# Two attentions of a transformer kernel: value products placed between the two banks of a step's second half of scores

## The chip, the cores and the metric

The kernel runs on one core of a Trainium2 chip. The metric is the device time of one execution in microseconds (us), as the median of several runs. TensorE (PE) multiplies matrices into PSUM, its accumulation memory of eight banks; VectorE (DVE), ScalarE (ACT) and GpSimd (POOL) do the elementwise work and the reductions; SyncE (SP) issues most DMAs. PEld is the loading of TensorE's weights. Each engine runs its own instructions in order and waits for the others at semaphores.

## The reference

The input x has 16 batches of 512 tokens with 128 features. Two layers follow each other, each an attention and a feed-forward part, with a layer norm ahead of each part and the sum with x behind it. Both attentions have 16 heads of 8 features; the first is causal, the second is not.

```python
    x = L0_attn_hidden_states
    x = x + _L0_attn_ref(_layernorm(x, axis=-1), ...)   # 16 heads, causal mask, projection
    x = x + _L0_ffn_ref(_layernorm(x, axis=-1), ...)    # 8 experts, the best 2 of each token
    x = x + _L1_attn_ref(_layernorm(x, axis=-1), ...)   # 16 heads, no mask
    x = x + _L1_ffn_ref(_layernorm(x, axis=-1), ...)    # gated, values rounded to a 4-bit grid

# an attention, q, k, v of shape (batch, head, token, 8):
        w = jnp.einsum('bhnd,bhmd->bhnm', q, k) * jax.lax.rsqrt(float(D))
        mask = jnp.tril(jnp.ones((S, S), dtype=jnp.float32))     # first attention only
        w = jnp.where(mask > 0, w, NEG)
        w = jax.nn.softmax(w, axis=-1)
        attn = jnp.einsum('bhnm,bhmd->bhnd', w, v)
```

## The kernel before, in words

One function, `attention(layer)`, emits both attentions. The 16 heads of a batch are worked off in 4 groups of 4 heads, so that there are 64 groups, and each group in NC = 4 steps, one for each block of 128 keys (`kc`). A count `now` runs over all 256 steps of an attention; a batch has 16 of them.

A step has the following parts. Every matmul of queries and keys uses 64 rows of PE's array: heads lie on two strips of 64 partitions, and the two strips (`j` = 0 and 1) go into two different PSUM banks. In the profile they are "64*128".

- `score(kc, pairs)` multiplies the keys of one block with the queries into two banks (`ps_sc`), one for each strip, and ACT takes the exponentials of each bank into `pt`. In the first attention POOL then clears what lies behind the mask (L981). `parts` cuts the scores of a step: two halves where two heads of a strip don't fit one bank, and a single part otherwise. In the second attention every step has two halves of 512 columns. In the first, step 0 has two halves of 512 columns and step 1 two of 384; steps 2 and 3 have a single part, of 2 x 256 and 2 x 128 columns.
- `row_max` computes the row maxima for the group that is LEAD = 3 groups ahead: PE writes the scores into two banks (`ps_max`), in the first attention adds a mask (a bf16 matmul with `ident_bf` and `mask_bf`, 128*128), and DVE reduces them (L923). A step's maxima come in the same one or two parts; the first of them is issued at the end of the step before, by `first_maxima`, the rest inside the step.
- `attend(kc)` is the value product of the step behind: four matmuls (`ps_av<-pt,va`, 128*32, which the profile counts as eight), one for each head of the group, each on its own 32 columns of PE's array. They accumulate in one bank over the four steps of a group. Behind the last of them `leave` lets ACT copy the bank to `av_sb`.
- `divide` turns the products of a finished group back (`ps_d`) at step 2 of the next group; DVE takes reciprocals and multiplies.
- Work for other batches is hung onto steps by number, in three tables: `soon` (ahead of the first maxima of a step), `later` (behind the first scores) and `last_of` (behind the last scores). It brings further PE operations: `ps_t`, `ps_qk`, `ps_v`, `ps_mx`, in the first attention also `ps_o` and `ps_n`.

The tiles `ps_sc`, `ps_av`, `ps_mx`, and in part `ps_t`, `ps_qk` and `ps_v`, take turns in a ring of 4 banks (`for_act`), one of which the value product of the group holds nearly all the time. `ps_max`, `ps_d` and the rest take turns in 2 buffers of two banks (`for_dve`).

The order on PE is that of the program: every matmul goes through `mm`, and `in_order` ties it to the one before. In the attentions the lanes of DVE, ACT and POOL are tied in the same way. The order within a step is written out in the loop at the end of `attention`: first scores, the divide (in the second attention it goes into `last_of`), `later`, the rest of the maxima, the second half of the scores, `last_of`, the first maxima of the next step, and the value products of the step behind. Where the second attention has something in `last_of` (`turned`), the products come ahead of the first maxima.

Of the kernel before, what the change touches and what calls it, by code (L numbers as in the profile page):

```python
# [36 lines left out]
def transformer_kernel(  # L37
# [25 lines left out]
    NC = S // P  # L63
# [79 lines left out]
    first = cp.tile([P, NE], F32, name="first")  # L143
# [8 lines left out]
    def in_order(ins, queue="pe", passing=False):  # L152


        if queue in last:
            tc.add_manual_dep(
                ins.ins, last[queue].name,
                mybir.DependencyInfo(
                    mybir.DependencyClass.NoSync, mybir.DependencyReason.DATA
                ),  # L160
                reason="in_order",
            )
        if not passing:
            last[queue] = ins.ins
        return ins
# [129 lines left out]
    def mm(out, lhsT, rhs, start=True, stop=True):  # L295
        return in_order(nc.tensor.matmul(out, lhsT, rhs, start=start, stop=stop))  # L296
# [320 lines left out]
    def attention(layer):  # L617
        causal = layer == 0
# [32 lines left out]
        def for_act(name):  # L651
            return ring["act"](name)
# [246 lines left out]
        def strip(j):  # L899
            return slice(64 * j, 64 * (j + 1))  # L900
# [52 lines left out]
        def main_parts(b, g):  # L953


            hv = halves[b, g // 2]
            va = state[b]["va"]
            pts = {}
            acc = {}

            def score(kc, pairs):
                q0 = kc * P if causal else 0
                n = S - q0
                m = len(pairs)
                tiles = [for_act("ps_sc") for j in range(2)]
                for u, i in enumerate(pairs):
                    p = 2 * (g % 2) + i
                    for j, ps in enumerate(tiles):
                        r = strip(j)
                        mm(  # L970
                            ps[:, u * n : (u + 1) * n],
                            hv["k"][r, p, kc * P : (kc + 1) * P], hv["q"][r, p, q0:S],
                        )
                for j, ps in enumerate(tiles):
                    pt = pool.tile([P, S], F32, tag="pt", name="pt", bufs=12 if causal else 8)
                    act.activation(pt[:, 0 : m * n], ps[:, 0 : m * n], AF.Exp, scale=SCALE)
                    if causal:

                        head = pt[:, 0 : m * n].rearrange("p (u n) -> p u n", u=m)[:, :, 0:P]
                        in_order(  # L980
                            nc.gpsimd.affine_select(  # L981
                                head, head, pattern=[[0, m], [1, P]], base=0,
                                channel_multiplier=-1, compare_op=ALU.is_ge, fill=0.0,
                            ),
                            queue="pool",
                        )
                    for u, i in enumerate(pairs):
                        pts[kc, i, j] = pt[:, u * n : (u + 1) * n]

            def attend(kc):  # L990
                if kc == 0:
                    acc[0] = for_act("ps_av")
                av = acc[0]
                q0 = kc * P if causal else 0
                for i in range(2):
                    for j in range(2):
                        s = 2 * j + i
                        mm(
                            av[32 * s : 32 * (s + 1), q0:S],
                            va[:, kc, NP * j + 2 * g + i, :],  # L1000
                            pts.pop((kc, i, j)),
                            start=kc == 0, stop=kc == NC - 1,
                        )

            def leave():
                t = pool.tile([P, S], F32, tag="av_sb", name="av_sb")
                act.copy(t, acc.pop(0))
                return t

            return score, attend, leave  # L1010

        def divide(b, g, t):

            st = state[b]
            if g == 0:
                st["at"] = pool.tile([P, NC, E], F32, tag="at", name="at")
            ps = for_dve("ps_d")[:, 0, :]
            for c in range(NC):
                cols = slice(c * P, (c + 1) * P)
                turn_to(ps[:, cols], t[:, cols])  # L1020
            p3 = ps.rearrange("p (n k) -> p n k", k=32)
            rec = pool.tile([P, NC * 4, 1], F32, tag="rec", name="rec")
            vec.reciprocal(rec, p3[:, :, D : D + 1])
            at = st["at"].rearrange("p c (j n d) -> p (c j) (n d)", j=2, d=D)
            vec.tensor_tensor(
                at[:, :, 2 * D * g : 2 * D * (g + 1)].rearrange("p m (i d) -> p m i d", d=D),
                p3[:, :, 0:D].rearrange("p (m i) d -> p m i d", i=2),
                rec.rearrange("p (m i) o -> p m i o", i=2).to_broadcast([P, NC * 2, 2, D]),
                ALU.mult,
            )  # L1030
# [32 lines left out]
        def parts(blocks):  # L1063

            return [(0, 1)] if causal and 2 * blocks * P <= S else [(0,), (1,)]

        def max_steps(n):
            if n >= len(groups):
                return []
            b, g = groups[n]  # L1070
            return [
                [(lambda c=c, u=u: row_max(b, g, c, u)) for u in parts(c + 1)]
                for c in reversed(range(NC))
            ]

        def max_done(n, step=None):
            if n < len(groups) and n % 2 == 1:
                at = groups[n][0], (n % G) // 2
                if step is None:
                    part_max(*at)  # L1080
                    put_max(*at)
                else:
                    soon.setdefault(step, []).append(lambda: part_max(*at))
                    later.setdefault(step + (not causal), []).append(lambda: put_max(*at))


        soon, later, last_of = {}, {}, {}
# [125 lines left out]
        behind, left = [], []  # L1213
# [77 lines left out]
        maxima = []  # L1291

        def first_maxima(now):

            for f in soon.pop(now, []):
                f()
            n, kc = divmod(now, NC)
            if kc == 0:
                rows[:] = max_steps(n + LEAD)
            if rows:  # L1300
                maxima[:] = rows.pop(0)
                maxima.pop(0)()
# [3 lines left out]
        for n, (b, g) in enumerate(groups):  # L1306
            nxt = n + LEAD
            score, attend, leave = main_parts(b, g)
            max_done(nxt, NC * (n + 1))
            for kc in range(NC):  # L1310
                now = NC * n + kc
                scores = [lambda u=u: score(kc, u) for u in parts(NC - kc)]
                scores.pop(0)()
                if kc == 2 and left:
                    bb, gg, t = left.pop(0)
                    if not causal:
                        last_of.setdefault(now, []).append(lambda a=(bb, gg, t): divide(*a))
                    else:
                        divide(bb, gg, t)
                    if gg == G - 1 and causal:  # L1320
                        later.setdefault(now + 1, []).append(lambda bb=bb: turn_back(bb))
                        at = now + 3
                        later.setdefault(at, []).append(lambda bb=bb: finish(bb))
                        gate_after(bb, at)
                    elif gg == G - 1:
                        later.setdefault(now + 1, []).insert(0, lambda bb=bb: finish(bb))
                        quantize_after(bb, now + 1)
                for f in later.pop(now, []):
                    f()
                for f in maxima + scores:  # L1330
                    f()
                maxima.clear()
                turned = now in last_of and not causal
                for f in last_of.pop(now, []):
                    f()
                if not turned:

                    first_maxima(now + 1)

                while behind:  # L1340
                    behind.pop(0)()
                if turned:
                    first_maxima(now + 1)
                behind.append(lambda kc=kc, f=attend: f(kc))
            behind.append(lambda b=b, g=g, f=leave: left.append((b, g, f())))
        while behind:
# [499 lines left out]
```

## Time and profile before

| What | Value |
|---|---|
| Median of 3 runs | 2224.25 us (2222.96 to 2224.55) |
| Profiled execution, device time | 2213.31 us |
| Its span, first to last instruction | 2211.6 us |
| Mean granted clock of PE | 0.958 |
| Busy share of the span: PE, PEld, DVE, ACT, POOL | 91%, 46%, 74%, 58%, 44% |
| Step scores in the first attention | 62.3 us to about 760 us |
| Step scores in the second attention | about 1180 us to 1970.7 us |

The two attentions take about two thirds of the span; experts stand between them, and the gated feed-forward part behind them. In the timeline a row is a start, a duration, an engine and an operation with the number of instructions merged into it. Durations of matmuls overlap with what follows, since their ends are modelled: from start to start is the safer reading. Nearly all work of the attentions goes through two helper lines (L296 for PE, L177 for the lanes of the other engines), so that groups have to be told apart by their tiles.

### The profile page before, as it was taken

What the parts mean: (1) busy time and instruction counts of PE and PEld (TensorE: products, weight loads), DVE (VectorE), ACT (ScalarE), POOL (GpSimd) and SP (SyncE); (2) the same over time, 40 slices, a digit from 0 to 9 for tenths busy, and PEclk for the clock granted to TensorE, in tenths of its full rate; (3) what the DMA queues carried; (4) which work ended last, traced back from release to release, by engine and by line L of the source; (5) the groups of instructions that cost most, each with busy time, mean ns of one, the idle gap of its engine ahead of it and who ended that gap; (6) DMA issues with size and microseconds to landing.
All of it is one profiled execution on the core that took longest, in us unless ns stands there. A gap on an engine that the chain in (4) does not pass through costs nothing.

```text
span 2211.6 us, 38195 instructions
## 1 busy us (share of the span) xinstructions
PE 2021.9 (91%) x13141; PEld 1026.8 (46%) x13141; DVE 1633.6 (74%) x3002; ACT 1288.7 (58%) x2549; POOL 979.4 (44%) x1593
## 2 busy tenths in 40 slices
PE   6999999999999939899998999999999999987887
PEld 3454444444444416565763333333333333335565
DVE  5777677777777666468637888888888888828776
ACT  1566666656666623323336777777777777763433
POOL 3454756657465750321204454554545552222331
PEclk6899999999999969999999999999999999998888
DMA  6521223222232024564542222222222222000000
GB/s 178 126 67 62 82 93 105 74 68 79 86 111 75 30 74 121 144 179 124 165 119 89 79 85 75 70 74 72 70 71 86 85 72 70 22 1 10 20 24 24
DMA packets 148735, 180.14 MB, mean 81 GB/s; under 512 B 25647, under 2 KB 112784, under 8 KB 140352
## 3 DMA queue, kind: packets, MB, share of 16 engines
q1 hardware_dynamic: 139614, 160.26, 24.1%
q0 software_dynamic: 8352, 17.20, 2.6%
q8 instruction: 105, 1.72, 0.3%
q14 instruction: 86, 0.70, 0.1%
q10 hardware_dynamic: 578, 0.26, 0.1%
HBM read 116.55 MB, written 58.99 MB: 79 GB/s over the span
## 4 chain that ended last, share of the span: by engine, by line
PE 43%; DVE 9%; ACT 4%; issue 1%; POOL 0%; DMA 0%; ACTq 0%; DVEq 0%; POOLq 0%
PE ps_av L296 11%; PE ps_sc L296 8%; PE ps_max L296 6%; PE ps_h L296 5%; PE ps_y L296 5%; DVE hid L177 4%; ACT pt L177 3%; PE ps_gu L296 3%; DVE mx L923 2%; PE ps_d L299 2%; PE ps_qk L296 2%; PE ps_t L299 1%; PE ps_mx L299 1%; PE ps_v L296 1%; DVE f_rc L177 1%
## 5 line engine op out<-in xcount | busy, mean ns | idle before, releaser
L177 ACT ACTIVATE pt<-ps_sc 128x512 f32<-128x512 f32 (+2 forms) x1792 | 895.4, 572 | 397.1 <-PE ps_sc L296 381.4
L923 DVE TENSOR_REDUCE mx<-ps_max 128x2 f32<-128x1024 f32 (+1 forms) x896 | 993.2, 1143 | 180.2 <-PE ps_max L296 175.6
L296 PE MATMUL ps_sc<-q,k 64*128 64x512 f32 (+3 forms) x2048 | 512.4, 424 | 41.0 <-ACT pt L177 38.7
L296 PE MATMUL ps_av<-pt,va 128*32 128x512 f32 (+3 forms) x4096 | 477.2, 528 | 7.1 <-POOL pt L981 7.0
L296 PE MATMUL ps_max<-k,q 64*128 64x512 f32 (+3 forms) x2048 | 435.2, 412 | 21.6 <-DVE mx L923 12.1
L296 PEld LDWEIGHTS ps_sc<-q,k 64*128 64x128 f32 x2048 | 234.8, 185 | 443.5 <-ACT pt L177 329.9
L981 POOL TENSOR_SCALAR_AFFINE_SELECT pt<-pt 128x128 f32<-128x128 f32 (+1 forms) x768 | 244.9, 331 | 237.6 <-ACT pt L177 221.5
L296 PEld LDWEIGHTS ps_max<-k,q 64*128 64x128 f32 x2048 | 202.1, 189 | 181.3 <-DVE mx L923 54.7
L1538 ACT ACTIVATE h<-ps_h,b1t 128x512 f32<-128x512 f32 x156 | 106.9, 687 | 185.9 <-PE ps_h L296 185.5
L1462 POOL DMA_INDIRECT got<-y_rows,backs x128 | 125.4, 979 | 99.5 <-DMA y_rows<-yt 65.1
L296 PE MATMUL ps_h<-xT,w1t 128*128 128x512 f32 x312 | 153.0, 623 | 13.3 <-ACT h L1538 8.0
L296 PE MATMUL ps_y<-w2t,h 128*128 128x128 f32 x1248 | 146.5, 276 | 0.8 <-DVE yt L1552 0.8
L296 PEld LDWEIGHTS ps_y<-w2t,h 128*128 128x128 f32 x1248 | 142.5, 192 | 3.2 <-issue 2.2
L296 PEld LDWEIGHTS ps_av<-pt,va 128*32 128x32 f32 x4096 | 83.7, 108 | 129.0 <-issue 61.0
L537 POOL DMA_INDIRECT x_rows<-xg,slots x128 | 127.6, 997 | 27.6 <-issue 25.0
L206 POOL TENSOR_TENSOR ln_rstd<-ln_ve,mhalf 128x4 f32<-128x4 f32 x62 | 64.2, 1035 | 157.8 <-DVE ln_nm L177 130.0
L296 PE MATMUL ps_max<-mask_bf,ident_bf 128*128 128x128 bf16 (+1 forms) x768 | 127.2, 249 | 0.0
L177 DVE RECIPROCAL rec<-ps_d 128x16 f32<-128x16 f32 x128 | 32.6, 255 | 108.3 <-PE ps_d L299 108.3
L177 POOL TENSOR_TENSOR hid<-hid,f_sc 128x1408 f32<-128x1408 f32 x16 | 41.4, 2587 | 136.5 <-DVE hid L177 136.5
L177 ACT ACTIVATE hid<-ps_gu 128x352 f32<-128x352 f32 x64 | 29.7, 463 | 123.0 <-PE ps_gu L296 123.0
L296 PE MATMUL ps_gu<-wgT,xqT 128*128 128x352 f32 x128 | 62.8, 579 | 41.1 <-DVE hid L177 41.1
L177 ACT COPY av_sb<-ps_av 128x512 f32<-128x512 f32 x128 | 75.2, 587 | 42.8 <-PE ps_av L296 42.3
(241 smaller groups left out, 2186.8 us busy)
## 6 DMA issues: line engine op xcount, KB each, us to landing
q<-d SPq DMA_DIRECT2D x256, 128.0 KB
k<-d SPq DMA_DIRECT2D x256, 128.0 KB
d<-hi SPq DMA_DIRECT2D x64, 256.0 KB
d<-lo SPq DMA_DIRECT2D x64, 256.0 KB
xt<-x_rows SPq DMA_DIRECT2D x39, 262.0 KB
w1t<-in_w_dram SPq DMA_DIRECT2D x39, 256.0 KB
w2t<-in_w_dram SPq DMA_DIRECT2D x39, 256.0 KB
y_rows<-yt SPq DMA_DIRECT2D x39, 256.0 KB
```

The costliest lines, as they stand in the source:

```text
L177: ins = f(*args, **kw)
L206: in_order(nc.gpsimd.tensor_tensor(rstd, ve, mhalf, ALU.pow), queue="pool")
L296: return in_order(nc.tensor.matmul(out, lhsT, rhs, start=start, stop=stop))
L299: return in_order(nc.tensor.transpose(out, src, ident))
L537: ins = in_order(nc.gpsimd.indirect_dma_start(out=x_rows[:, :], out_offset=bass.IndirectOffsetOnAxis(ap=slots[:, b0 + u, k, c : c + 1], axis=0
L923: nc.vector.tensor_reduce(hv["mx"][:, c, :, p0 : p0 + m], s4, AX.X, ALU.max),
L981: nc.gpsimd.affine_select(head, head, pattern=[[0, m], [1, P]], base=0, channel_multiplier=-1, compare_op=ALU.is_ge, fill=0.0,),
L1462: ins = in_order(nc.gpsimd.indirect_dma_start(out=got[:, c, :], out_offset=None, in_=y_rows[0 : min(NT, NE * (b + 1)) * TS, :], in_offset= ...
L1538: nc.scalar.activation(h[:, f, :], ps, AF.Gelu, bias=t["b1"][:, f : f + 1])
```

## The change

In steps with two halves, the second half of the scores is issued one bank at a time, and the value products of the step behind (`attend`, and `leave` behind the last step of a group) are put between the two banks. Then come `last_of` and the first maxima of the next step. In steps with a single part (steps 2 and 3 of the first attention) the order stays: first maxima, then value products. The special order of `turned` is gone: in the second attention the divide now stands behind the value products, and the first maxima follow it directly. `score` gets an argument for the strips that it computes.

```diff
-            def score(kc, pairs):
+            def score(kc, pairs, strips=(0, 1)):
...
-                tiles = [for_act("ps_sc") for j in range(2)]
+                tiles = [(j, for_act("ps_sc")) for j in strips]
                 for u, i in enumerate(pairs):
                     p = 2 * (g % 2) + i
-                    for j, ps in enumerate(tiles):
+                    for j, ps in tiles:
...
-                for j, ps in enumerate(tiles):
+                for j, ps in tiles:
...
-                scores = [lambda u=u: score(kc, u) for u in parts(NC - kc)]
-                scores.pop(0)()
+                first, *second = parts(NC - kc)
+                score(kc, first)
...
-                for f in maxima + scores:
+                for f in maxima:
                     f()
                 maxima.clear()
-                turned = now in last_of and not causal
+                woven = bool(second)
+                for u in second:
+                    score(kc, u, (0,) if woven else (0, 1))
+                sums, behind[:] = list(behind), []
+                if woven:
+                    for f in sums:
+                        f()
+                    for u in second:
+                        score(kc, u, (1,))
                 for f in last_of.pop(now, []):
                     f()
-                if not turned:
-                    first_maxima(now + 1)
-                while behind:
-                    behind.pop(0)()
-                if turned:
-                    first_maxima(now + 1)
+                first_maxima(now + 1)
+                if not woven:
+                    for f in sums:
+                        f()
```

## The prediction

> **What bounds the kernel now.** I read the page's sections 1 and 4 first, then the table of windows, the waits, and last the timeline of TensorE (PE) inside single steps.
>
> ```profile
> PE 2021.9 (91%) x13141; PEld 1026.8 (46%) x13141; DVE 1633.6 (74%) x3002; ACT 1288.7 (58%) x2549; POOL 979.4 (44%) x1593
> ...
> PE 43%; DVE 9%; ACT 4%; issue 1%; POOL 0%; DMA 0%; ACTq 0%; DVEq 0%; POOLq 0%
> ```
>
> PE is the busiest engine and carries the chain; no DMA stands in it. By stage, from the windows (us; PE, PEld, DVE, ACT, POOL busy):
>
> ```profile
> 400.00:700.00 300.00, 288.99 (x2322) 143.19 (x2320) 223.61 (x503) 188.26 (x416) 184.76 (x429) 0.99 0.26 82
> 1500.00:1750.00 250.00, 239.35 (x1464) 95.65 (x1462) 215.51 (x332) 191.45 (x370) 129.45 (x144) 1.00 0.24 77
> ```
>
> First attention: PE 96%, VectorE (DVE) 75%. Second: PE 96%, but DVE 86%, so little can come off PE there before DVE ends last. Clocks are full. The waits (us, times, longest):
>
> ```profile
> PEld ps_av L296 <- POOL pt L981: 30.8, 89, 2.0
> PE ps_sc L296 <- ACT pt L177: 38.7, 149, 4.5
> PE ps_max L296 <- DVE mx L923: 12.1, 35, 1.1
> ```
>
> The second is the wait the change aims at: the last bank of a step's scores waits for an exponential to free one. An ordinary step of the second attention (start, duration):
>
> ```profile
> 1600.36 1.06 PE L296 MATMUL ps_av<-pt,va 128*32 128x512 f32 x8
> 1601.36 0.50 PE L296 MATMUL ps_sc<-q,k 64*128 64x512 f32 x2
> ...
> 1601.70 0.39 PE L296 MATMUL ps_max<-k,q 64*128 64x512 f32 x2
> ...
> 1601.93 0.39 PE L296 MATMUL ps_sc<-q,k 64*128 64x512 f32 x1
> ...
> 1602.54 0.49 PE L296 MATMUL ps_sc<-q,k 64*128 64x512 f32 x1 [0.21 <-ACT pt L177]
> ...
> 1602.54 0.72 PE L296 MATMUL ps_max<-k,q 64*128 64x512 f32 x2
> ...
> 1603.19 1.07 PE L296 MATMUL ps_av<-pt,va 128*32 128x512 f32 x8
> ```
>
> Read start to start, since modelled ends overlap. A pair of 64-row matmuls (one on each half of the array's rows) takes 0.23 (1601.70 to 1601.93), but 0.34 as the first behind the value products (1601.36). The bank wait is 1601.93 to 1602.54, 0.61 less the 0.23 of the matmul: 0.38. And at 1602.54 the late half starts together with the first maximum: a lone half finds a partner.
>
> The first attention, steps 0 and 1 of a group:
>
> ```profile
> 325.36 0.54 PE L296 MATMUL ps_sc<-q,k 64*128 64x512 f32 x2
> 325.69 0.39 PE L296 MATMUL ps_max<-k,q 64*128 64x384 f32 x2
> 326.01 0.28 PE L296 MATMUL ps_max<-mask_bf,ident_bf 128*128 128x128 bf16 x2
> 326.23 0.43 PE L296 MATMUL ps_av<-pt,va 128*32 128x128 f32 x8
> ...
> 315.92 0.45 PE L296 MATMUL ps_sc<-q,k 64*128 64x384 f32 x2
> 316.20 0.50 PE L296 MATMUL ps_max<-k,q 64*128 64x256 f32 x4
> 316.64 0.39 PE L296 MATMUL ps_max<-mask_bf,ident_bf 128*128 128x256 bf16 x2
> 316.96 1.07 PE L296 MATMUL ps_av<-pt,va 128*32 128x512 f32 x8
> ```
>
> Here PE runs without a gap and no bank wait stands: 0.33, 0.32, 0.22, then the products.
>
> **The change part by part.** No instruction is added or removed; DVE, POOL and SP (with its DMA issues) keep their orders. On PE the four ps_av products move ahead of bank 1 of the second half and of the next first maxima, in 64 x 4 steps of the second attention and 64 x 2 (steps 0 and 1) of the first. On ACT the copy of a finished group (0.49 to the next) moves ahead of one exponential (0.52): hidden, since ACT is busy 77% and 63%; uncovered it would be 64 x 0.5 us in each attention.
>
> *First attention, PE's own work.* No row shows a half with other modes on both sides. The nearest is one ps_sc whose weights load uncovered, ahead of ps_d: 0.42 (1595.81 to 1596.23); a half that finds all hidden takes 0.23. I take 0.43 (0.34 as the first, 0.1 for the switch out); with 0.23 the parts below shrink to about a half. Step 0 before: 0.33 + 0.32 + 0.22 + 0.35 (products) = 1.22. After: bank 0 alone 0.43, products 0.35, bank 1 with the first maximum 0.34, second maximum 0.17 + 0.11 for the switch = 0.28, mask 0.22: 1.62, so +0.40. Step 1 before: 0.28 + 0.44 (four maxima) + 0.32 + 1.00 = 2.04; after: bank 0 alone 0.39 (384 columns instead of 512), products 1.00, bank 1 and the four maxima 0.62 (five halves, 0.28 for the first two slots' start, then 0.23 and the switch of 0.11), mask 0.32: 2.33, so +0.29. Together 0.7 a group; 61 groups still have maxima: **+43 us**.
>
> *Against it.* In two of four groups step 0 does wait between second scores and maxima (357.21 to 358.37 is 1.16 where 0.33 is due). There the moved products fill the wait and 0.40 isn't lost: 2 x 0.4 x 15 batches = **-12 us**.
>
> *Waits moved.* Step 1's products need step 0's masked exponentials from POOL and now come 0.44 (the four maxima) + 0.32 (mask) earlier, with bank 1's scores and the maxima queued behind them. Once in two batches they already stall (1.1 us at 363.28); after it, 0.94 of maxima and mask are still to run, 0.55 more than counted. In about four more such steps in two batches POOL is in a 1.0 us x_rows DMA issue: about 0.3 each. (0.55 + 1.2) / 2 x 15 = **+13 us** (bounds 0, if POOL keeps ahead, and 30, all 61 at 0.5). Step 1 issues its maxima 1.00 later, so step 2's divide and last maxima may wait for DVE's two buffers: 0 to 0.3 in half the groups, **+4 us**.
>
> *Second attention.* A batch is four groups of four steps and takes 50.6 (1587.43 to 1638.05, ps_av to ps_av). An ordinary step turned on 1.18 (first scores to the freed bank, 1601.36 to 1602.54) + 0.65 + 1.00 = 2.83. After, bank 1 comes first behind the products and shares with a maximum, maxima share with scores, and the wait reappears at the next step's bank 0 of the second half: its bank is the one bank 1's exponential frees, again 1.18 later. Then 0.34 to 0.43 to the products and 1.00: 2.52 to 2.61. With seven such steps a batch: 7 x -0.22 to -0.31 = -1.5 to -2.2. In the four steps with a divide (ps_d) both halves stand alone, bank 0 ahead of the products (0.34), bank 1 between them and ps_d (0.43), where a pair took 0.34: +0.43 each, less the 0.38 of wait that two of them had: +1.0. There the products also no longer run while DVE divides (reciprocal and product, 0.5), so what is late next is DVE's reduce of the next maxima, by up to that; two maxima buffers ahead of it let PE go on. Six times a batch ps_mx, ps_qk, ps_t or ps_v stand inside, with an odd number of halves on each side. Before: scores 0.44, maxima 0.33, scores 0.23, maxima 0.34, 1.34 in all; after: 0.34 + 0.23 + 0.33 (one score alone, and the switch) ahead of the operation, maxima 0.34 and bank 0 0.34 behind it, 1.58: +0.24 each, +1.4. Sum +0.2 to +0.9 a batch; I take the lower end, since DVE (86%) hides some of PE's extra, times 15: **+3 us**.
>
> *A rule that speaks against the change.* The row: two maxima and two scores, four halves, take two slots of 0.23. The Trainium skill, TensorE: Matmul & The Clock Gate, "Part 3: Packing small matmuls", says that matmuls on different rows of the array run at once and that a pack takes about one matmul's time; a half alone then wastes a slot. By the rule alone, splitting costs 256 x 0.23 + 64 x (0.23 + 0.17) = 85 us. The trace at 1602.54 lets the half pair across tiles, so I charge it only where a mode change isolates it.
>
> Sum: 43 - 12 + 13 + 4 + 3 = +51. The profiled execution took 2213.3 (span 2211.6, 1.7 around it), giving 2264; it was 10.9 faster than the median 2224.25, so 2224 + 51 = **2275 us**.
>
> **The rivals.**
> *Waits absorb it* (chance 0.16). PE's waits in the first attention (bank and DVE) exceed what I credit, and POOL's and DVE's new ones (17) don't come. 43 - 24 - 5 = +14: 2238. For it: 1.69 at 312.52. Against: the shown steps, without a gap.
> *The freed bank comes in time* (0.09), the other side: if exp-to-bank takes under 0.8 from bank 1's scores (the place of the next bank 0, 0.34 + 0.23 + 0.23 later), the 0.38 wait vanishes in nine steps a batch: 9 x 0.38 x 15 = -51; with the first attention at 31 and no new waits, -20: 2204. Against: 1.18 was needed at 1602.54, and DVE at 86%.
> *Pairing fails* (0.08): DVE makes maxima late or the sequencer keeps halves apart: +0.23 in some 240 steps, +55 on top: 2330.
> *It doesn't do what it says*: PE's order has the products between the banks in all 384 steps; excluded.
>
> **How the numbers follow.** The main case has 0.67, from +25 (POOL and DVE waits nil) to +85 (upper bounds). Range 2235 to 2312: it leaves out most of the faster case and of failed pairing. Resolution is about 0.2%, 4.4 us. Faster 0.09, within 0.04, slower 0.87.
>
> **What would show it.** Right: the first attention's batches longer by some 3 us (45 to 46.4 now), the second's 50.6 nearly unchanged; ordinary steps there near 2.55 with the wait on bank 0, divide steps longer; more wait of ps_av on POOL. Wrong: lone halves of step 0 at 0.33 or less to the products (then the 43 fails); ordinary steps at 2.83 (no gain) or near 2.2 (wait gone).

## The result and the profile after

The changed kernel takes 2274.94 us (2269.33 to 2292.25, four runs), the kernel before 2223.61 (2221.83 to 2224.55, four runs): slower, ratio 1.024, 95% interval 1.0207 to 1.0272. The prediction said 2275. Measured a second time, beside before at 2217.57, the same kernel took 2254.34, ratio 1.0175 (1.0155 to 1.0196). The two intervals don't overlap. By the medians the loss is 51 us the first time and 37 the second; where most of the 14 us between them lie is found below.

The first profiled execution took 2269.33 (span 2267.6, clock 0.961), 56.0 more than that of before. Cut at the first and last `ps_h` of the experts and the last step scores, the 56.0 fall into first attention +44.6, experts +2.5, second attention +8.5, and +0.4 behind it. The page, sections 1 and 4:

```profile
PE 2070.3 (91%) x13141; PEld 1042.0 (46%) x13141; DVE 1638.3 (72%) x3002; ACT 1305.8 (58%) x2549; POOL 980.8 (43%) x1593
...
PE 44%; DVE 9%; ACT 2%; issue 1%; POOL 0%; DMA 0%; ACTq 0%; DVEq 0%; POOLq 0%
```

PE has the same 13141 instructions and is busy 48 us longer (2021.9 before): a half that stands alone counts as busy time like a pair, although it uses only 64 of the array's 128 rows. The chain is PE's still. The two windows of the prediction:

```profile
400.00:700.00 300.00, 286.61 (x2181) 139.80 (x2180) 207.40 (x461) 180.97 (x392) 176.05 (x405) 0.99 0.26 79
1500.00:1750.00 250.00, 240.61 (x1444) 95.23 (x1440) 213.86 (x329) 191.75 (x367) 128.16 (x141) 1.00 0.25 77
```

In the first attention a batch takes 47.9 to 50.6 us, some 3 more than before, and 300 us now hold 2181 matmuls instead of 2322, with PE hardly less busy. The waits, over the whole span (us, times, longest):

```profile
PE ps_sc L296 <- ACT pt L177: 12.1, 20, 4.5
PE ps_max L296 <- DVE mx L923: 15.9, 46, 1.1
PEld ps_av L296 <- POOL pt L981: 37.7, 98, 2.3
```

The wait that the change aims at fell from 38.7 to 12.1. The others rose, by 3.8 and 6.9. The list of waits got shorter, and the kernel 51 us slower. The first attention, from bank 0 of step 0's second half (349.74) over step 1 (first scores at 351.34) to the start of step 2 (start, duration):

```profile
349.74 0.50 PE L296 MATMUL ps_sc<-q,k 64*128 64x512 f32 x1
350.17 0.43 PE L296 MATMUL ps_av<-pt,va 128*32 128x128 f32 x8
350.53 0.49 PE L296 MATMUL ps_sc<-q,k 64*128 64x512 f32 x1
...
351.13 0.29 PE L296 MATMUL ps_max<-mask_bf,ident_bf 128*128 128x128 bf16 x2
351.34 0.44 PE L296 MATMUL ps_sc<-q,k 64*128 64x384 f32 x2
...
352.11 0.44 PE L296 MATMUL ps_sc<-q,k 64*128 64x384 f32 x1
352.48 1.22 PE L296 MATMUL ps_av<-pt,va 128*32 128x512 f32 x8
353.63 0.44 PE L296 MATMUL ps_sc<-q,k 64*128 64x384 f32 x1
353.63 0.67 PE L296 MATMUL ps_max<-k,q 64*128 64x256 f32 x4
354.23 0.39 PE L296 MATMUL ps_max<-mask_bf,ident_bf 128*128 128x256 bf16 x2
354.56 0.50 PE L296 MATMUL ps_sc<-q,k 64*128 64x256 f32 x4
354.99 0.66 PE L299 MATMUL ps_d<-cst,av_sb 128*128 128x128 f32 x4
355.94 0.44 PE L296 MATMUL ps_max<-k,q 64*128 64x128 f32 x4 [0.30 <-DVE mx L923]
```

Bank 0 alone takes 0.43 in step 0 (349.74 to 350.17) and 0.37 in step 1 (352.11 to 352.48). Step 1's bank 1 starts together with the maxima at 353.63, and the five halves take 0.60. New against before is the last row: from `ps_d` to the next maximum 0.95, of which 0.30 is a wait for VectorE's reduce. Before, that stretch took 0.58 in the same group.

An ordinary step of the second attention, and one with a divide ahead of it:

```profile
1585.93 1.06 PE L296 MATMUL ps_av<-pt,va 128*32 128x512 f32 x8
1586.93 0.49 PE L296 MATMUL ps_sc<-q,k 64*128 64x512 f32 x1
1587.35 0.66 PE L299 MATMUL ps_d<-cst,av_sb 128*128 128x128 f32 x4
...
1589.40 1.07 PE L296 MATMUL ps_av<-pt,va 128*32 128x512 f32 x8
1590.40 0.49 PE L296 MATMUL ps_sc<-q,k 64*128 64x512 f32 x1
1590.40 0.72 PE L296 MATMUL ps_max<-k,q 64*128 64x512 f32 x2
1590.74 0.61 PE L296 MATMUL ps_sc<-q,k 64*128 64x512 f32 x2
1591.50 0.50 PE L296 MATMUL ps_max<-k,q 64*128 64x512 f32 x2
1591.84 0.39 PE L296 MATMUL ps_sc<-q,k 64*128 64x512 f32 x1
1592.16 1.07 PE L296 MATMUL ps_av<-pt,va 128*32 128x512 f32 x8
```

Bank 1 finds a partner where a first maximum follows (1590.40), and stands alone for 0.42 ahead of `ps_d` (1586.93 to 1587.35). This ordinary step takes 2.76, most take 2.61.

### The profile page after: what moved, and what is told of

It is laid out like the page before. It is cut to its first block, busy times and chain, and to the rows that moved or that the text cites. A ratio compares the mean times of both kernels' runs of the same rounds, so it can differ in the third digit from the quotient of the medians.

```text
span 2267.6 us, 38195 instructions
## 1 busy us (share of the span) xinstructions
PE 2070.3 (91%) x13141; PEld 1042.0 (46%) x13141; DVE 1638.3 (72%) x3002; ACT 1305.8 (58%) x2549; POOL 980.8 (43%) x1593
## 4 chain that ended last, share of the span: by engine, by line
PE 44%; DVE 9%; ACT 2%; issue 1%; POOL 0%; DMA 0%; ACTq 0%; DVEq 0%; POOLq 0%
PE ps_av L296 10%; PE ps_sc L296 10%; PE ps_max L296 6%; PE ps_h L296 5%; PE ps_y L296 5%; DVE hid L177 4%; PE ps_gu L296 3%; DVE mx L923 2%; PE ps_d L299 2%; PE ps_qk L296 2%; ACT pt L177 1%; PE ps_t L299 1%; PE ps_v L296 1%; PE ps_mx L299 1%; DVE f_rc L177 1%
## 5 line engine op out<-in xcount | busy, mean ns | idle before, releaser
L923 DVE TENSOR_REDUCE mx<-ps_max 128x2 f32<-128x1024 f32 (+1 forms) x896 | 1006.3, 1144 | 246.2 <-PE ps_max L296 202.1
L177 ACT ACTIVATE pt<-ps_sc 128x512 f32<-128x512 f32 (+2 forms) x1792 | 916.5, 571 | 437.7 <-PE ps_sc L296 393.4
L296 PE MATMUL ps_sc<-q,k 64*128 64x512 f32 (+3 forms) x2048 | 590.7, 412 | 13.4 <-ACT pt L177 12.1
L296 PE MATMUL ps_max<-k,q 64*128 64x512 f32 (+3 forms) x2048 | 494.7, 421 | 30.8 <-DVE mx L923 15.9
L296 PE MATMUL ps_av<-pt,va 128*32 128x512 f32 (+3 forms) x4096 | 482.5, 528 | 10.8 <-POOL pt L981 10.1
L296 PEld LDWEIGHTS ps_sc<-q,k 64*128 64x128 f32 x2048 | 272.1, 185 | 444.1 <-ACT pt L177 262.1
L296 PEld LDWEIGHTS ps_max<-k,q 64*128 64x128 f32 x2048 | 224.4, 188 | 164.3 <-issue 62.6
L296 PEld LDWEIGHTS ps_h<-xT,w1t 128*128 128x128 f32 x312 | 51.4, 193 | 90.2 <-ACT h L1546 59.6
```

The lines of the kernel that those rows point to most:

```text
L177: ins = f(*args, **kw)
L923: nc.vector.tensor_reduce(hv["mx"][:, c, :, p0 : p0 + m], s4, AX.X, ALU.max),
```

## Experiments

Each kernel was timed in five rounds beside the kernel before; "ratio" is to before, with its 95% interval. Where a kernel uses the new order in some steps only, the other steps keep the old order whole.

**The parts alone.** New order in the first attention only:

```diff
-                woven = bool(second)
+                woven = bool(second) and (causal)
```

> The new order in the first attention alone; the second as before. My theory: the loss is made in the first attention (lone halves of scores, maxima that share with them, and ps_d ahead of a late DVE buffer), +43 to +47 us against before, and the traces' +45 there is no effect of the second. Rival: the two attentions' costs are tied to each other through the work hung onto the steps and the routing between them; then this gives clearly less than +40.

Measured: 2266.07 against 2218.77, ratio 1.021 (1.019 to 1.023), +47.3 us; the second attention's batches take 50.62 as before. As expected.

New order in the second attention only:

```diff
-                woven = bool(second)
+                woven = bool(second) and (not causal)
```

> The new order in the second attention alone; the first as before. My theory: the gains of ordinary steps (2.84 to 2.61 us) and the losses of steps with a divide or another PE operation nearly cancel, +7 to +12 us against before. Rival: DVE, 86% busy there, is what costs, and ends last whatever PE does; then +20 us or more.

Measured: 2210.60 against 2218.77, ratio 0.9949 (0.993 to 0.9969), -8.2 us. The sign is against the expectation: a batch takes 50.02 instead of 50.62. The two parts sum to +39, not to the +51 of the first measurement.

**The changed kernel once more**, to see which of the two sums holds.

> The changed kernel unaltered, run again beside the kernel before. In its first profile the second attention's batches took 51.3 to 52.2 us, with one or two steps a batch 0.6 to 1.5 us longer than the same steps of the version with the new order in the second attention alone (50.02 a batch), although the second attention's program is the same. If that excess belongs to the combination, it comes again: ratio 1.022 to 1.027, batches above 51. If it belonged to that one execution, batches come back to 50.0 and the time to about 2219 + 47 - 8 = 2258, ratio 1.018.

Measured: 2254.34 against 2217.57, ratio 1.0175 (1.0155 to 1.0196): +37 by the medians, near the sum of the parts. From first to last step scores the second attention takes 788.9 us, against 806.3 in the first profile; the first attention's batches are the same within 0.3 but for the first one. Behind its first step, the second attention of the two executions agrees step by step within 0.03 us, except for the fifth and the twelfth step of the batch, which in most batches of the first execution were longer by 0.6 and by 0.6 to 1.4. ScalarE's timeline in a fifth step, first execution:

```profile
1595.68 0.58 ACT L177 ACTIVATE pt<-ps_sc 128x512 f32<-128x512 f32 x1
1597.46 2.07 ACT L177 ACTIVATE pt<-ps_sc 128x512 f32<-128x512 f32 x4 [1.19 <-PE ps_sc L296]
```

and the same step in the repeat:

```profile
1586.17 0.58 ACT L177 ACTIVATE pt<-ps_sc 128x512 f32<-128x512 f32 x1
1587.26 2.06 ACT L177 ACTIVATE pt<-ps_sc 128x512 f32<-128x512 f32 x4 [0.51 <-PE ps_sc L296]
```

PE had started these scores at 1596.24 and at 1586.73, both 0.56 behind the start of ScalarE's row above; the exponential follows 1.22 behind them in the one execution and 0.53 in the other. Something like it also appears where the second attention is not changed: in the two kernels below with the new order in step 0 or in step 1 of the first attention only, measured side by side, the second of a batch's two steps with `ps_mx` took about 3.3 in the mean, where the profile of before has 2.93, and the batches took 51.0. These steps lie beside POOL's gathers of `y_rows`, but the same gathers stand there in the executions without the stall. The chip alone is not it: the kernel with the new order in the whole first attention ran on the same chip as these two, earlier, and has no stall (50.62). The cause stays open, and no run tried it.

**Which steps of the second attention.** New order only in the eight steps of a batch that have neither a divide nor another operation of PE:

```diff
-                woven = bool(second)
+                woven = bool(second) and (not causal and now % 16 in (0, 1, 3, 4, 8, 11, 12, 15))
```

> The first attention as before. In the second, the new order only in the 8 of 16 steps of a batch that hold neither a divide nor ps_mx, ps_t, ps_qk or ps_v; the other steps as before. My theory: only halves cut off by another tiling cost; with those steps left out, some 7 steps a batch gain 0.22 us each, -1.5 us a batch, -15 to -24 us in all (2200 to 2209). Rival: the bank wait only moves from one step to the next, or DVE takes the gain back; then within 5 us of before.

Measured: **2177.78** against 2218.77, ratio 0.9816 (0.9798 to 0.9835), -41 us: about twice the expectation, and faster than both kernels. A batch takes 47.98. The step behind a divide, in this kernel:

```profile
1408.06 1.06 PE L296 MATMUL ps_av<-pt,va 128*32 128x512 f32 x8
1409.05 0.50 PE L296 MATMUL ps_max<-k,q 64*128 64x512 f32 x2
1409.39 0.39 PE L296 MATMUL ps_sc<-q,k 64*128 64x512 f32 x2
1409.62 0.40 PE L296 MATMUL ps_max<-k,q 64*128 64x512 f32 x2
1409.85 0.38 PE L296 MATMUL ps_sc<-q,k 64*128 64x512 f32 x1
1410.16 0.64 PE L296 MATMUL ps_av<-pt,va 128*32 128x512 f32 x4
```

and the end of the same step in the kernel before (it began with its products at 1419.97):

```profile
1421.77 0.38 PE L296 MATMUL ps_sc<-q,k 64*128 64x512 f32 x1
1422.38 0.49 PE L296 MATMUL ps_sc<-q,k 64*128 64x512 f32 x1 [0.23 <-ACT pt L177]
1422.79 0.50 PE L296 MATMUL ps_max<-k,q 64*128 64x512 f32 x2
1423.22 0.64 PE L296 MATMUL ps_av<-pt,va 128*32 128x512 f32 x4
```

2.10 instead of 3.25. Bank 1's wait and the maxima behind it are no longer ahead of the products, and as the step before had the old order, no lone half was left over to this step's start. What is put off is paid at the end of a run of such steps: the last of them, ahead of an old-order step, takes for example 3.50 instead of 2.93.

New order only in the four steps with a divide, `now % 16 in (2, 6, 10, 14)`:

> The new order only in the second attention, and there only in its four steps of a batch that have a divide. By the prediction's terms each costs 0.43 less 0.38 of wait in two of them, +1.0 a batch, +15 us. If the 33 us between the version with the new order in the whole second attention (-8) and the one without divide steps and other-operation steps (-41) all lie in the divide steps: +25 to +33. If they lie in the steps with ps_mx, ps_qk, ps_t or ps_v: within 5 us of before.

Measured: 2222.86 against 2217.57, ratio 1.0025 (1.0015 to 1.0035), +5.3 us. The third number came nearest, and the prediction's +15 was too much. VectorE's waits from 1300 to 1800 us, in the kernel before:

```profile
DVE mx L923 <- PE ps_max L296: 59.8, 79, 1.1
DVE rec L177 <- PE ps_d L299: 4.7, 20, 0.2
```

and with the new order in the divide steps:

```profile
DVE rec L177 <- PE ps_d L299: 38.0, 39, 1.0
DVE mx L923 <- PE ps_max L296: 32.3, 40, 1.1
```

VectorE now idles 1.0 ahead of each divide, since `ps_d` stands behind the products, but nearly as much less for the maxima: 70.3 in both rows together, 64.5 before. The delay of the divide mostly takes the place of idle time that was there.

New order only in the steps with another operation and no divide, `now % 16 in (5, 7, 9, 13)`:

> The new order only in the second attention, and there only in the four steps of a batch in which ps_mx, ps_qk or ps_t stands among the scores and that have no divide. By the prediction's term, 0.24 each: 4 x 0.24 x 15 = +14 us. If the parts add (whole second attention -8, the eight steps with neither -41, the four divide steps +5): +28. Rival: these steps have their operation as cover for a bank's wait, so nothing is lost: within 5 us of before.

Measured: 2235.57 against 2225.48, ratio 1.0037 (1.0023 to 1.005), +8 us by the ratio and +10 by the medians: between the rival's 5 and the prediction's +14, and far from the sum's +28. A batch takes 51.5 to 51.6. Against the 50.62 of before's profile that would be the prediction's +14, but in this measurement before took 2225.48, and the two other kernels measured with it, whose second attention has the old order, took 51.0 a batch with the longer step described above. Against these it is 0.57 a batch, or +8.5. The three subsets give -41, +5 and +8 to +10, about -27 in all, and the whole -8. They don't add. What follows is a reading of step lengths that no run tested by itself. Each border between an old-order step and a new-order step behind it has a short step, as in the fence above; with the new order everywhere there are no such borders.

**Where the first attention loses.** Step 0 of every second group only (`causal and kc == 0 and n % 2 == 0`), groups in which PE waits between second scores and maxima:

> The second attention as before. In the first, the new order only in step 0 of every second group, the one without ps_mx, where PE waited between the second scores and the maxima (0.97 to 1.69 us where 0.33 is due). My theory: the moved products fill a wait there, so this costs nothing or gains, 0 to -15 us against before. Rival: a lone half costs 0.4 us there as elsewhere and the wait is DVE's and stays; then +8 to +15 us.

Measured: 2221.08 against 2218.77, ratio 1.0007 (0.9993 to 1.002). Steps 0 and 1 together take 5.36 in such a group, 3.20 + 2.16 before and 1.88 + 3.48 now: the products are early by 1.3 and all of it comes back in the step behind. The wait moved, and nothing clear of the noise was gained or lost.

Step 0 of all groups (`causal and kc == 0`), and step 1 of all groups (`causal and kc == 1`):

> The new order only in the first attention and only in step 0 of each group. By the prediction: own work 61 x 0.40 = +24, less the filled waits, 12: +12 us. If the waits in half the groups are VectorE's and only move to the next step, as the run with the even groups alone showed (nothing gained, nothing lost), the other 30 groups pay 0.40 each: again about +12. Rival: the lone half is covered everywhere, 0.

> The new order only in the first attention and only in step 1 of each group. By the prediction's sizes: own work 61 x 0.29 = +18, POOL +13, VectorE's buffers +4: +35. By the terms as the two traces measured them: +18, POOL 4, the wait of ps_d 16 x 61/48 = 20: +42, less what makes the sum with step 0 exceed 47: about +35 too, but with ps_d to the next maximum at 0.85 and the products' wait on POOL hardly longer. Rival: step 0 carries most, and this alone costs under 20.

Measured: 2240.83 against 2225.48, ratio 1.0068 (1.0054 to 1.0082), +15.4, for step 0; 2267.03, ratio 1.0189 (1.0169 to 1.021), +41.6, for step 1. Step 1 carries most. The two sum to 57 and don't add either: the new order in both steps costs 47. From `ps_d` to the next operation it takes 0.84 in the mean of ten batches with step 1 alone (0.53 before) and 0.54 with step 0 alone, so that wait belongs to step 1's order. One detail missed: the products of 512 columns, which here wait for POOL, take longer than expected. In the whole batches that ran at full granted clock they cost 9 us more than before for 61 groups, and 7 with the new order in both steps.

**Is it VectorE's buffer?** In the first attention `ps_d` takes a bank of ScalarE's ring (it has four banks; the expectation below says six), so that it needs none of the two maxima buffers; in the changed kernel and in the kernel before:

```diff
-            ps = for_dve("ps_d")[:, 0, :]
+            ps = for_act("ps_d") if causal else for_dve("ps_d")[:, 0, :]
```

> The changed kernel, but in the first attention the divide's transposes (ps_d) take a bank of the ring of six that ScalarE's tiles use, not one of VectorE's two maxima buffers. Theory: in the new order step 1's maxima are issued behind the products, so step 2's ps_d waits for a buffer; that wait is 16.0 of the 34.9 us that twelve batches gained. Then the stretch from ps_d to the next maximum falls from 0.86 to about 0.55 us and the kernel gets 15 to 20 us faster than the change, 2255 to 2260. Rival: the wait is VectorE's pace and only moves to the next maximum or, by the taken bank, to the next scores: less than 5 us.

> The same move of ps_d in the kernel before. Theory: there ps_d finds its buffer free (0.53 us to the next operation), so nothing is gained: within 0.2% of before. Rival: a buffer more for the maxima helps in any order: 5 to 15 us faster.

Measured: 2251.12, against 2254.34 for the changed kernel beside it: 3 us, where 15 to 20 were expected. In before: 2216.21 against 2217.57, ratio 1.0004 (0.9989 to 1.0019), nothing. The waits from 150 to 710 us in the changed kernel:

```profile
PEld ps_av L296 <- POOL pt L981: 25.2, 67, 2.3
PEld ps_max L296 <- DVE mx L923: 23.5, 57, 0.8
```

and with the other bank:

```profile
PEld ps_av L296 <- POOL pt L981: 27.3, 77, 2.3
PEld ps_max L296 <- DVE mx L923: 14.0, 33, 0.7
```

The wait for VectorE fell by 9.5, as the theory had it. Why did so little of it reach the total? The windows from 150 to 710 us, first of the changed kernel and then with the other bank, and one stretch of the latter (us; busy times of PE, PEld, DVE, ACT, POOL; the third number from the end is the granted clock):

```profile
150.00:710.00 560.00, 536.25 (x4109) 261.94 (x4107) 387.88 (x851) 339.24 (x736) 322.08 (x752) 0.99 0.26 79
150.00:710.00 560.00, 544.42 (x4122) 265.72 (x4118) 393.83 (x852) 343.43 (x741) 319.98 (x752) 0.98 0.26 81
432.10:438.90 6.80, 6.80 (x28) 3.34 (x27) 3.64 (x11) 2.43 (x5) 2.23 (x8) 0.50 0.00 0
```

In the profile with the other bank the clock was halved in five stretches of 3.4 or 6.8 us of this window, 23.8 in all; in that of the changed kernel in one, 6.8. So sums over all batches mix the bank with the clock. Nine batches of the first attention ran at full clock throughout both in this profile and in the repeat of the changed kernel. With the other bank each of them is shorter, by 0.7 to 1.5 and 0.85 in the mean, which is 13 us for 61 groups: 14.5 less from `ps_d` to the next operation, 1.7 more on the products of 512 columns, and the rest nearly cancels. At full clock the theory of the buffer thus holds, a little short of its 15 to 20. In the medians 3 us are left (6 by the ratios), with a mean granted clock of 0.950 to 0.964 in the five runs, against 0.950 to 0.961 in those of the changed kernel. Whether the other bank brings on the halved stretches, or they fell there by chance, was not tested, and each figure by batches rests on one profiled execution. The rival, that the wait only moves, is not what the full-clock batches show.

**Maxima ahead of the products.** New order in the first attention only, but bank 0, first maxima, products, bank 1:

```diff
-                woven = bool(second)
+                woven = bool(second) and causal
...
+                turned = now in last_of and not causal
+                for f in last_of.pop(now, []):
+                    f()
+                if not turned:
+                    first_maxima(now + 1)
+                for f in sums:
+                    f()
                 if woven:
-                    for f in sums:
-                        f()
                     for u in second:
                         score(kc, u, (1,))
-                for f in last_of.pop(now, []):
-                    f()
-                first_maxima(now + 1)
...
```

> The new order only in the first attention, with one difference: the next step's first maxima stand ahead of the products (bank 0, first maxima, products, bank 1). If late maxima are what makes step 1 dear (ps_d waiting for VectorE's buffer, and the waits at ScalarE and POOL that came in its place when ps_d had another bank), that goes and only the lone halves' own work stays: bank 0 with the maxima 0.60, mask 0.22 or 0.32, products 0.36 or 1.00, bank 1 joined to the next step's scores 0.23: 1.41 against 1.22 and 2.15 against 2.04, 61 x 0.3 = +18 us. Rival: it is the late bank 1, whose exponentials the products of the step after wait for through POOL, that costs: as with the new order in the first attention alone, +40 to +47.

Measured: 2232.65 against 2216.33, ratio 1.007 (1.0056 to 1.0083), +16 us, against +47 with the maxima behind the products. Steps 1 and 2 of a group:

```profile
355.63 1.07 PE L296 MATMUL ps_av<-pt,va 128*32 128x512 f32 x8
356.62 0.67 PE L296 MATMUL ps_sc<-q,k 64*128 64x384 f32 x5
357.22 0.66 PE L299 MATMUL ps_d<-cst,av_sb 128*128 128x128 f32 x4
357.71 0.64 PE L299 MATMUL ps_t<-cst,xn 128*128 128x128 f32 x4
358.29 0.44 PE L296 MATMUL ps_max<-k,q 64*128 64x128 f32 x4
```

Bank 1 joins the next step's four halves (0.60 for five; four take 0.44), and behind the divide no wait for VectorE stands; from `ps_d` to the next operation it takes 0.55 in the mean of ten batches, as before (0.53). Some 31 of the 47 us of the first attention hang on the maxima's place behind the products; the split of the banks in this order costs the rest, 16.

But this order changes two things: VectorE gets its maxima earlier, and bank 1 shares with scores instead of maxima. The ten batches at full clock both here and with the new order in the first attention alone tell them apart. Scaled to 61 groups they differ by 39: 19 from `ps_d` to the next operation, 8 on the products of 512 columns, which in the first attention wait for POOL, 13 on PE's scores and maxima themselves, and -1 elsewhere. So about half of what the maxima's place costs is the wait at `ps_d`, the one that the other bank mostly removed. (At full clock this order costs 11 against before; its profile, too, has more halved stretches than that of before.)

## Why the prediction was right, and where its terms were not

**The total.** 2224 + 51 = 2275 against 2274.94. That they agree to a tenth of a microsecond is luck. The change by its parts is +39 (+47 and -8), and the repeat gives +37. The rest of the +51 goes with the stalled steps in the second attention (17 us in the profiled execution), which no step of the prediction contained. Against the repeat, the sum was 14 us too high. The direction, the place of the loss and most of the rows were forecast; the sizes of the terms were not, and their errors cancelled in part.

**First attention, predicted +48, measured +47.** The terms, from the time between an operation and the next, summed over 12 batches (48 groups) of the first two profiles (556.4 to 591.3 us, +34.9) and scaled to 61 groups:

| Term | Predicted | 48 groups | Scaled |
|---|---|---|---|
| PE's own work: lone halves and maxima apart | +43 | +24.9 | +32 |
| waits filled | -12 | -8.5 | -11 |
| products wait for POOL | +13 | +3.4 | +4 |
| VectorE's buffers, behind `ps_d` | +4 | +16.0 | +20 |
| all else | 0 | -0.9 | -1 |

The own work of +24.9 is 7.75 and 8.0 on the maxima of 256 and 384 columns and, by the rows, 0.19 a group for the two lone halves; the filled waits are what is left of the scores' change of +0.6, so that the split between these two rows is an estimate. The rows themselves came as forecast: bank 0 alone 0.43 and 0.37, step 0 at 1.60 in all (1.62 predicted), step 1 at 2.30 (2.33). By the rows this is 0.64 a group, or 39 for 61 groups; the sum's 32 would mean that not every group paid in full.

**The term that was mis-sized: "step 2's divide and last maxima may wait for DVE's two buffers: 0 to 0.3 in half the groups".** The wait was seen and sized at 4; it is 20 in the trace, nearly as much as PE's own work. It stands in three of four groups, where `ps_d` to the next operation takes 0.95 and took 0.49 to 0.59 before. That it is the buffer is shown at full clock: with another bank for `ps_d` 14.5 of it go, and 13 reach the sum. With the maxima ahead of the products it goes altogether. What is not shown is why the rest of the late maxima's price, at POOL's products and in PE's own slots, goes with the order too.

**POOL's wait** at step 1 exists (the longest went from 2.0 to 2.3) but was put at two to three times its size: 4 by the table, 7 by the batches at full clock. "In two of four groups step 0 does wait" was right, and the credit of 12 is near what the table shows. The run with those products alone agrees: +2 us, within its noise, where 0.40 in each of those groups would be 12. But the wait was moved there and not filled: the products came 1.3 earlier, and the step behind took 1.3 longer.

**Second attention, predicted +3, measured -8 alone.** Ordinary steps "2.52 to 2.61": 2.61. Per batch, step lengths against the prediction's terms: four ordinary steps -1.19 (-1.04 by the terms), three steps with `ps_mx` or `ps_qk` +0.50 (+0.72), the two pairs of a divide step with another operation and its follower +0.77 (+0.82), the pair with a plain divide -0.35 (-0.21), the pair of divide and `ps_t` -0.17 (+0.29), the last step of the batch -0.16 (0). In sum -0.60 instead of +0.58 (of which the prediction took +0.2): every term was a little too dear, most of all the pair with `ps_t`, for which VectorE's waits in the divide steps suggest a reason: the late divide takes the place of idle time. The wait for bank 0 did reappear, 1.18 behind bank 1's scores (1617.04 to 1618.22 in one step), as reckoned.

**The rivals.** "Waits absorb it" has its place in the table's second row and no more. "The freed bank comes in time" did not occur: with the new order everywhere the bank is again needed 1.18 behind bank 1's scores. In the eight chosen steps no bank wait stands in the step of 2.10 and the kernel is 41 us faster, but there the step before had the old order and left no bank 1 behind, which is not the rival's way. "Pairing fails" did not occur: bank 1 pairs with a maximum at the same start wherever one follows.

**The rule on packing** overstated the price, as the prediction held: by a slot of its own for each lone half it gave 85 us; the halves paired across tiles, the own work in the first attention came to about 32, and the second attention lost nothing.

## What to carry to other kernels

A matmul moved ahead to fill a wait also delays what it moves past: follow the maxima (or whatever feeds another engine) as far as that engine's next result, not only PE's own slots. A wait that goes from the list is a gain only if the next operation isn't waiting for the same late engine: in every second group of the first attention products moved into a wait came 1.3 us earlier, and all of it came back in the step behind. Compare profiles where the clock is the same: at first sight the other bank for `ps_d` had moved its wait elsewhere, and most of that was the clock. Try an order step by step: the same rewrite was worth -41 us in eight steps of the batch and -8 in all sixteen.

## What the runs showed of the hardware that was not expected

The changed kernel, unaltered, took 2.4% more than before in one measurement and 1.75% in another, with the same granted clock of 0.961 in both profiles. In the first, two steps of nearly every batch of the second attention had an exponential 0.7 later behind its scores than in the repeat, 17 us in all; what held it was not found. Differences of half a per cent between kernels that were not measured side by side say little here, even where each interval is narrower. Behind its first batch the first attention of the two executions agreed within 0.3 us a batch, of about 50. Profiles of different kernels differ in one thing more: stretches of 3.4 or 6.8 us at half the granted clock, 6.8 us of them between 150 and 710 us in the changed kernel and 23.8 with the other bank for `ps_d`.

A half of the array's rows pairs with the half of the other strip that stands next in the queue, across tiles and accumulations: bank 1 and a maximum start together at 353.63, four halves of 256 columns take 0.44, and with one of 384 ahead of them 0.60. A half alone between operations of the whole array takes 0.37 (384 columns) to 0.43 (512), more than a pair that has others of its kind behind it, 0.28 to 0.34.
